# Moving GpSimd's last biases, products and sum ahead of VectorE's last split of maxima, with a new order of stores and products in the tail

## The chip, the cores and the metric

The kernel runs on one core of a Trainium2 chip. The metric is the device time of one execution in microseconds (us); a kernel is judged by the median of several executions. One further execution was taken with the hardware profiler: its span runs from its first to its last instruction, and its own time is a little longer than its span.

## The reference

A residual attention layer whose queries and keys are shifted by a projected condition; 8 batches, 512 rows, width 512, 16 heads of 32, all in float32:

```python
Q = split_heads(x @ Wq.T + bq); K = split_heads(x @ Wk.T + bk); V = split_heads(x @ Wv.T + bv)
tQ = split_heads(tokens @ Wq.T + bq); tK = split_heads(tokens @ Wk.T + bk)   # tokens = cond[:, None, :]
scores = einsum('bhqd,bhkd->bhqk', Q + tQ, K + tK) / sqrt(32)
attn = softmax(scores, axis=-1)
out = x + merge_heads(einsum('bhqk,bhkd->bhqd', attn, V))
```

## The kernel before, in words

**Steps.** The work is cut into T = 32 steps; step t is batch t // 4 and a group of four heads t % 4. A step needs, for its 128 rows of q and k (four heads of 32), the scores of 512 queries by 512 keys, their row maxima, exponentials, row sums (the denominators), and the product with V. The projections of the next batch (each product is made from seven smaller block products, as in Strassen's scheme) are spread over the steps as filler for TensorE. The main loop (L1236, function `thirds`) handles steps 1 to 28, in three thirds each. The last three steps, 29, 30 and 31, are written out by hand from L1294 to the end.

**Maxima.** The scores of step t+1 are first computed with queries on the partitions, and VectorE reduces them to negated row maxima (`nmax`, L589, L650, L1289). Before the scores of that step can be computed a second time with keys on the partitions, the maximum has to be added inside TensorE's sum. So `split_max` (L710 to L719) splits each float32 maximum into three bfloat16 pieces by four tiny dependent instructions on 128x16 elements: a cast (L716), a difference (L717), a cast (L718), a difference (L719). In the main loop GpSimd does them; for steps 30 and 31 VectorE does (L1325, L1359). Then the pieces are transposed, by a DMA (`turn_max`, L728) in the loop or by TensorE (`transpose_max`, L738, and a copy, L744) at the end, and enter the scores as a small matmul (L754, L775, L1269). Only then can step t's scores (L757, L786, L1272), the exponentials of ScalarE (L767, L796, L1287) and the products with V (L801, L817) follow.

**Kept exponentials.** For steps 1 to 29 half of the exponentials of the first computation are kept (`kept`) and turned, so that they need not be computed again: VectorE transposes 32x32 blocks (`turn_kept`, L660), and DMAs from SBUF to SBUF exchange six pairs of blocks by three moves each (`swap_kept`, L665 to L683): move 0 sets one block aside, move 1 copies its partner into its place, move 2 brings the block that was set aside into the partner's place. The n-th pair's move goes to GpSimd's own DMA queue or to SyncE's, by the condition `here`. `halves_of` (L817) multiplies the turned half with V, so it needs all moves of its step.

**The residual.** `load_residual` (L182 to L196) brings x's block for a step by four DMAs of SyncE (L191); for step 31 it only points at the transposed x that is already in SBUF. `bias_residual` (L198 to L204) adds V's bias on GpSimd. `send` (L886 to L894) transposes a step's sum on VectorE (L889), multiplies by the reciprocal of the denominator on GpSimd (L890), adds the residual on GpSimd (L891) and stores by four DMAs of SyncE (L894). `send_sums` puts VectorE's reciprocal (L1049) ahead of it.

**What sets the order.** TensorE, ScalarE, VectorE and GpSimd run the instructions in the order in which the program names them; an instruction that waits holds up all that stand behind it on its engine. SyncE's queue alone is ordered by the planner of the tile framework, from its own costs and due times, under the same dependences.

**The end by hand, before the change.** In step 29's part (L1295 to L1336): last maxima of step 30, moves 1 and 2 of the swap of step 29, the products of steps 28 and 29, VectorE's split for step 30, `send_sums(28)`, `load_residual(29)`. In step 30's part: three stretches `crossed` (L1255 to L1292), each with the maxima of step 31 for 128 queries and the scores of step 30 for 128 keys, and between them `load_residual` of 30, `bias_residual` of 31 and 29, the product and the sums of 29, GpSimd's half of the first sum of exponentials (`sum_of`, L1353, L1244), `send_sums(29)`, `bias_residual(30)`. Then comes VectorE's split for step 31 (L1359), the last one. From there on each chunk of keys is one stretch of scores, exponentials, products with V and VectorE's sums (L1244, L1246), to the denominators by `times_ones` (L827).

**The tail.** Step 30's result (`y30`) is transposed on VectorE (L1390), multiplied and added on GpSimd (L1392, L1393) and stored by four DMAs (L1398). Step 31's is kept transposed: VectorE multiplies the residual with the denominators in two halves (L1411, L1413; between them ScalarE copies the denominators, L1412), adds the product with V (L1422), TensorE transposes (L898, L1424), and VectorE divides (L1427, L1432) and two DMAs store the halves (L1438), the first on ScalarE's queue and the second on SyncE's.

Of the kernel before, what the change touches and what calls it, by code (L numbers as in the profile page):

```python
# [12 lines left out]
ALU = mybir.AluOpType  # L13
# [4 lines left out]
def kernel(  # L18
# [163 lines left out]
    def load_residual(t):  # L182

        b, g = divmod(t, G)
        if turned_by_vector(t):
            if t >= T - 3:
                xr[t] = late[0][:, (t - T + 3) * 4, :].rearrange("p (f e) -> p f e", e=BL)
            else:
                xr[t] = op.tile([P, NB, BL], F32, tag="xr", name=f"xr_{t}")
            for h in range(HG):  # L190
                nc.sync.dma_start(  # L191
                    xr[t][h * BL : (h + 1) * BL], spread(x[b], g * P + h * BL)
                )
        else:

            xr[t] = xT[b][:, g, :]  # L196
# [465 lines left out]
    APART = [(a, g) for a in range(HG) for g in range(a + 1, HG)]  # L662
    between = store[:, 16:18]

    def swap_kept(t, move, last=nc.gpsimd):  # L665

        later = 6 if t % 4 == 1 else 2

        def part(a, g):
            return kept[t][a * BL : (a + 1) * BL, g].rearrange("p c h s -> p (c h s)")  # L670

        for n, (a, g) in enumerate(APART):
            at = (n + 2) % HG * BL
            aside = (store[:, 6:8] if t == KEPT[-1] else between)[at : at + BL, n // HG]
            aside = aside.rearrange("p i s -> p (i s)")
            to, of = [(aside, part(a, g)), (part(a, g), part(g, a)), (part(g, a), aside)][move]
            if t < KEPT[-2]:
                here = move == 2 or move == 0 and n >= later
            elif t < KEPT[-1]:
                here = move == 2 and n < 3 or move == 0 and n >= later  # L680
            else:
                here = n >= 3
            (last if here else nc.sync).dma_start(to, of)  # L683

    def denominators(t, qc, w=HG, js=range(HG)):

# [36 lines left out]
    def turn_max(t):  # L723

        if t >= T:
            return
        maxT[t] = op.tile([P, S], BF16, tag="maxT", name=f"maxT_{t}")
        nc.sync.dma_start_transpose(  # L728
            maxT[t].rearrange("p (c q) -> p c q", c=NS),
            split[t % 2].rearrange("p c h e -> p (c h e)"),  # L730
        )
# [398 lines left out]
    def thirds(t, made):  # L1130

        b, r = divmod(t, G)
        of = (t - 1) // G + 1
        begin(0, HG)
        turn_more(t, 0, 0)
        row_max_aside(t + 1, 1)
        max_aside(t + 1, 1)
        row_max(t + 1, 2, False, HG)
        turn_more(t, 0, 1)
        denominators(t + 1, 1, None, (1, 2, 3, 0))  # L1140
        denominators(t + 1, 2, HG)
        weighted(t - 1, banks(0), banks(1), nothing)
        turn_more(t, 0, 2)
        load_blocks()
        one_item(of, *next(made), (2, 3), ignore, nothing)
        released(0, 1, 4, 5, 6, 7, 2, 3)
        for i in (1, 2):
            begin(HG)
            exponentials_of_rest(t, i - 1)
            turn_more(t, i, 0)  # L1150
            rows = (t + 1, 3) if i == 1 else (t + 2, 0)
            row_max(*rows, False, HG)
            turn_more(t, i, 1)
            if i == 1:
                swap_kept(t, 2)
                split_max(t + 1)
                turn_max(t + 1)
            dens = lambda js=range(HG): denominators(*rows, HG, js)
            n, u, kind = next(made)
            if kind == "first":  # L1160
                products(of, n, u, kind, False, dens, nothing, None)
                turn_more(t, i, 2)
            elif n == "v":
                small = nothing
                if t + 1 not in KEPT:
                    small = lambda: transpose_max(t + 1, banks(2), nc.scalar.copy)
                other_shared(of, n, u, dens, (0, 3), small, lambda: turn_more(t, i, 2))
                released(1, 2, 4, 5, 6, 7, 0, 3)
            else:
                products(of, n, u, kind, False, dens, nothing, False)  # L1170
                turn_more(t, i, 2)
            if i == 1:
                aparts[t] = masked(t)
            load_blocks()
            if (t + 1, i) == (KEPT[-1], 1):
                swap_kept(t + 1, 0)
            if i == 2:
                if r == 0:
                    combine_x(b + 1, 1, nc.gpsimd)
                if t + 1 < KEPT[-1]:  # L1180
                    load_residual(t + 1)
            else:
                if t > 1:
                    bias_residual(t)
                if r == 0:
                    combine_x(b + 1, 0, nc.gpsimd)
            if i == 2 and t + 1 < KEPT[-1]:
                for move in range(2):
                    swap_kept(t + 1, move)
# [35 lines left out]
    def one_item(b, n, u, product, at, dens, last):  # L1225
# [7 lines left out]
        else:  # L1233
            other_products(n, b, u, dens, nothing, at, True)

    for t in KEPT[:-1]:  # L1236
        thirds(t, iter(MADE[(t - 1) % G * 3 :]))
    places[:] = *range(8, 16), *range(4), 16, 17
# [52 lines left out]
            )  # L1291
        row_max_of(u, qc, 1, banks(HG + 2, 2))  # L1292

    late.append(store[:, 4:8].rearrange("p c i s -> p (c i) s"))  # L1294
    t = T - 3  # L1295
    begin(0, HG)
    first, second = row_of[0][:HG], row_of[0][HG:]
# [12 lines left out]
    swap_kept(t, 1)  # L1310
    apart = masked(t - 1)
    aparts[t] = masked(t)
    swap_kept(t, 2)
    halves_of(t - 1, banks(0), (1,))
    row_of[0] = [*second[:2], *first[2:], *first]
    exponentials_of_rest(t, 0)
# [14 lines left out]
    halves_of(t, banks(0), (1,), (2, 3))  # L1331
    nc.scalar.copy(whole[t][:, HS:], banks(0)[:, HS:])
    send_sums(t - 1, whole[t - 1], den)
    load_residual(t)
    at_end[:] = [*row_of[0][HG:], first[1], first[0], first[3], second[0]]
    row_of[0] = None  # L1336

# [1 line left out]
    row(0)  # L1339
    crossed(t, 0, 1)  # L1340
    apart = masked(t - 1)
    for u in (t, t + 1):
        load_residual(u)
    for u in (t + 1, t - 1):
        bias_residual(u)
    halves_of(t - 1, banks(2), (0,))
    nc.scalar.copy(whole[t - 1][:, :HS], banks(2)[:, :HS])
    spread_sums(apart, banks(1))
    den = denominators_of(t - 1, banks(1))
    row(1)  # L1350
    crossed(t, 1, 2)
    acc = room_for_sums(t)
    sum_of(t, acc, 1, nc.gpsimd, [1])  # L1353
    part_of(t, banks(2), [0])
    send_sums(t - 1, whole[t - 1], den)
    bias_residual(t)
    row(2)
    crossed(t, 2, 3)
    split_max(t + 1, nc.vector)  # L1359
# [29 lines left out]
    y30 = op.tile([P, NB, BL], F32, tag="res", name=f"res_{t - 1}")  # L1389
    nc.vector.transpose(y30.rearrange("p f e -> p (f e)"), parts[t - 1])  # L1390
    x30 = xr.pop(t - 1)
    nc.gpsimd.tensor_tensor(y30, y30, rec.broadcast_to([P, NB, BL]), ALU.mult)  # L1392
    nc.gpsimd.tensor_tensor(y30, y30, x30, ALU.add)  # L1393

    def store_30(queue, hs):
# [1 line left out]
        for h in hs:  # L1397
            queue.dma_start(spread(out[b], g * P + h * BL), y30[h * BL : (h + 1) * BL])  # L1398

    store_30(nc.sync, (0, 1, 3))  # L1400
    exponentials(t, 3, (4, 2, 0, 1))
    times_v(t, 2, pv)
    pd = bank(7)
# [6 lines left out]
    two = [slice(0, HS), slice(HS, S)]  # L1410
    nc.vector.tensor_tensor(part_x[:, two[0]], pd[:, two[0]], xr[t][:, two[0]], ALU.mult)  # L1411
    nc.scalar.copy(den, pd)  # L1412
    nc.vector.tensor_tensor(part_x[:, two[1]], pd[:, two[1]], xr[t][:, two[1]], ALU.mult)  # L1413
    store_30(nc.scalar, (2,))
    oT = late[0][:, 2, :]
    y = late[0][:, 1, :].rearrange("p (c s) -> p c s", c=NS)
    rec = op.tile([P, NS, HG, 1], F32, tag="rec", name="rec")
    pi, po = bank(6), [bank(4), bank(2)]
# [1 line left out]
    untranspose(den, pi)  # L1420
    for i in range(2):
        nc.vector.tensor_tensor(oT[:, two[i]], pv[:, two[i]], part_x[:, two[i]], ALU.add)  # L1422
        for qc in (i * 2, i * 2 + 1):
            nc.tensor.transpose(  # L1424
                po[i][:, qc * P : (qc + 1) * P], oT[:, qc * P : (qc + 1) * P], ident
            )
# [45 lines left out]
```

## Time and profile before

| | us |
|---|---|
| median of 3 runs | 659.02 (658.79 to 660.39) |
| the profiled execution's own time | 658.57 |
| its span | 656.8 |
| TensorE busy | 646.9 (98%) |
| VectorE busy | 600.8 (91%) |
| ScalarE busy | 534.6 (81%) |
| GpSimd busy | 431.1 (66%) |

In the profile PE is TensorE's matmul, PEld its weight load, DVE VectorE, ACT ScalarE, POOL GpSimd, SP SyncE; a q behind an engine's name is its sequencer, which issues DMAs. A line of the timeline has start and duration in us, engine, source line, operation, tile written and tiles read with their shapes, the count that was merged and, in brackets, the idle time before it with what ended it. The span lies 1.8 us inside the execution's own time, and the execution is 0.45 us below the median of the three runs.

### The profile page before, as it was taken

How to read it: one execution, taken by the hardware profiler on the slowest of the kernel's cores; microseconds unless marked ns; L12 is line 12 of the kernel's file. 1: busy time of each engine (PE TensorE's matmuls, PEld its weight loads, DVE VectorE, ACT ScalarE, POOL GpSimd, SP SyncE). 2: the span in 40 equal slices, each digit the busy share in tenths (PEclk: the TensorE clock that was granted, in tenths of full speed). 3: DMA queues.
4: the chain of work that ended last, by engine and by line, in shares of the span. 5: the costliest groups of instructions: out<-in, count | busy, mean ns of one | idle time of the engine just before them, and what ended most of it. 6: DMA issues, size and time to landing. Idle time of an engine off the chain costs nothing.

```text
span 656.8 us, 24923 instructions
## 1 busy us (share of the span) xinstructions
PE 646.9 (98%) x9856; PEld 349.5 (53%) x9856; DVE 600.8 (91%) x832; ACT 534.6 (81%) x1364; POOL 431.1 (66%) x680
## 2 busy tenths in 40 slices
PE   9999999999999999999999999999999999999977
PEld 7355455555555555555555555555555555555522
DVE  4799999999999999999999999999999989899897
ACT  2579888889888888988888898888898888887544
POOL 3633665796766777678757667677676776674651
PEclk9999999999999999999999999999999999999989
DMA  7633698988876787877898777787888767687521
GB/s 189 107 49 59 136 182 159 170 175 180 184 158 158 151 186 172 187 156 165 173 194 166 166 164 171 167 180 150 190 190 182 176 146 163 157 148 185 142 46 33
DMA packets 248458, 102.02 MB, mean 155 GB/s; under 512 B 229963, under 2 KB 230475, under 8 KB 248341
## 3 DMA queue, kind: packets, MB, share of 16 engines
q1 hardware_dynamic: 234724, 65.60, 52.6%
q0 software_dynamic: 12384, 33.83, 19.1%
q8 instruction: 78, 1.28, 0.9%
q10 hardware_dynamic: 1232, 0.98, 0.5%
q14 instruction: 40, 0.32, 0.2%
HBM read 19.75 MB, written 8.39 MB: 43 GB/s over the span
## 4 chain that ended last, share of the span: by engine, by line
PE 97%; DVE 1%; DMA 1%; issue 0%; ACT 0%; SPq 0%; DVEq 0%
PE psum L461 44%; PE psum L641 19%; PE psum L817 16%; PE psum L786 8%; PE psum L775 3%; PE psum L404 2%; PE psum L801 2%; PE psum L757 1%; DMA store<-in_x_dram 1%; PE psum L827 0%; PE psum L754 0%; DVE split L718 0%; PE psum L911 0%; PE psum L1272 0%; PE psum L313 0%; PE psum L852 0%
## 5 line engine op out<-in xcount | busy, mean ns | idle before, releaser
L702 ACT ACTIVATE store<-psum,nmax 128x512 f32<-128x512 f32 x204 | 140.1, 701 | 36.0 <-DVE nmax L589 26.3
L702 ACT ACTIVATE psum<-psum,nmax 128x512 f32<-128x512 f32 x248 | 164.7, 669 | 3.6 <-DVE nmax L589 3.0
L683 POOL DMA_DIRECT2D store<-store x258 | 128.7, 502 | 58.4 <-DMA store<-store 40.7
L589 DVE TENSOR_REDUCE nmax<-psum 128x1 f32<-128x512 f32 x225 | 144.4, 678 | 19.0 <-PE psum L641 16.8
L650 DVE TENSOR_REDUCE nmax<-psum 128x2 f32<-128x1024 f32 x125 | 151.4, 1211 | 0.0
L641 PE MATMUL psum<-kT,qT 32*128 32x512 f32 x1024 | 142.5, 617 | 0.0
L796 ACT ACTIVATE store<-psum 128x512 f32<-128x512 f32 x232 | 119.8, 602 | 26.7 <-PE psum L786 26.7
L660 DVE STREAM_TRANSPOSE store<-store 128x1024 f32<-128x1024 f32 x116 | 138.8, 1216 | 0.0
L817 PE MATMUL psum<-store,v 128*32 128x256 f32 x1856 | 106.8, 381 | 0.0
L817 PEld LDWEIGHTS psum<-store,v 128*32 128x32 f32 x1856 | 57.0, 110 | 57.1 <-ACT wT_q L628 21.2
L890 POOL TENSOR_TENSOR res<-res,recs 128x512 f32<-128x512 f32 x30 | 31.4, 1046 | 66.8 <-DVE res L889 66.7
L641 PEld LDWEIGHTS psum<-kT,qT 32*128 32x128 f32 x1024 | 55.7, 183 | 35.5 <-issue 20.0
L786 PE MATMUL psum<-qT,kT 32*128 32x256 f32 x928 | 59.9, 373 | 0.0
L702 ACT ACTIVATION_READ_ACCUMULATOR psum<-psum,nmax 128x1 f32 x248 | 52.7, 213 | 0.0
L461 PE MATMUL psum<-wc_v,xc 128*32 128x256 f32 x768 | 47.7, 379 | 0.0
L786 PEld LDWEIGHTS psum<-qT,kT 32*128 32x128 f32 x928 | 45.5, 184 | 3.9 <-issue 0.3
L204 POOL TENSOR_TENSOR xr<-xr,bvs 128x512 f32<-128x512 f32 x29 | 37.1, 1280 | 11.4 <-DMA x<-in_x_dram 11.4
L461 PE MATMUL psum<-xc,wc_k 128*32 128x256 f32 x720 | 44.5, 379 | 0.0
L461 PE MATMUL psum<-xc,wc_q 128*32 128x256 f32 x720 | 44.5, 379 | 0.0
L702 ACT ACTIVATION_READ_ACCUMULATOR store<-psum,nmax 128x1 f32 x204 | 43.9, 215 | 0.0
L891 POOL TENSOR_TENSOR res<-res,xr 128x512 f32<-128x512 f32 x29 | 37.1, 1278 | 2.3
L461 PE MATMUL psum<-xT,wT_k 128*32 128x256 f32 x480 | 34.5, 382 | 0.0
(196 smaller groups left out, 1001.4 us busy)
## 6 DMA issues: line engine op xcount, KB each, us to landing
store<-store SPq DMA_DIRECT2D x264, 128.0 KB, 2.6
store<-store POOLq DMA_DIRECT2D x258, 128.0 KB, 3.5
out_dram<-res SPq DMA_DIRECT2D x123, 64.0 KB, 3.6
xr<-in_x_dram SPq DMA_DIRECT2D x116, 64.0 KB, 3.0
x<-in_x_dram SPq DMA_DIRECT2D x112, 64.0 KB, 3.4
w_q<-in_L_cond_Wq_dram SPq DMA_DIRECT2D x4, 256.0 KB, 3.9
w_v<-in_L_cond_Wv_dram SPq DMA_DIRECT2D x16, 64.0 KB, 2.4
w_k<-in_L_cond_Wk_dram SPq DMA_DIRECT2D x16, 48.0 KB, 2.6
```

Source lines behind the costliest of these rows:

```text
L204: nc.gpsimd.tensor_tensor(xr[t], xr[t], bias, ALU.add)
L461: nc.tensor.matmul(pt[r], still[:, r], moving, start=(kc == kcs[0]), stop=(kc == kcs[-1]))
L589: nc.vector.tensor_reduce(nmax[t][:, qc, j : j + 1, 0], pt, AX.X, ALU.max, negate=True)
L641: nc.tensor.matmul(pt, qkT["q", t][r, qc * P : (qc + 1) * P], qkT["k", t][r, :], start=True, stop=True,)
L650: nc.vector.tensor_reduce(nmax[t][:, qc, pr * 2 : pr * 2 + 2, 0], pt, AX.X, ALU.max, negate=True)
L660: nc.vector.transpose(e, e)
L683: (last if here else nc.sync).dma_start(to, of)
L702: nc.scalar.activation(to, of, AF.Exp, bias=nmax[t][:, qc, j, :], accum_out=sums[t][:, qc, j, :],)
L786: nc.tensor.matmul(bank[j][:, i * HS : (i + 1) * HS], qkT["k", t][r, kc * P : (kc + 1) * P], qkT["q", t][r, rest], start=False, stop=(i == 1),
L796: nc.scalar.activation(e[:, i, :], bank[pr * 2 + i], AF.Exp)
L817: nc.tensor.matmul(pt[j * HD : (j + 1) * HD, half * HS : (half + 1) * HS], vs[b % 2][:, kc, (g * HG + j) * HD : (g * HG + j + 1) * HD], e, ...
L891: nc.gpsimd.tensor_tensor(y, y, xr.pop(t), ALU.add)
```

## The change

- **Residuals.** Step 29's residual gets a tile of the ordinary pool, and its load stands in the main loop's last pass; step 30's gets another place (row 2 of the late room, not row 4), and its load stands behind the swap of step 29. The output of step 31 before the transpose takes row 4 instead.
- **Biases.** `bias_residual(31)` and `bias_residual(29)` stand in step 29's part, ahead of and behind move 2 of its swap. `bias_residual(30)` stands at the end of that part, behind `send_sums(28)`.
- **Product of step 29.** `send_sums(29)` stands one `crossed` earlier, ahead of GpSimd's sum.
- **Swaps.** All six pairs' move 2 of step 28 goes to GpSimd's queue, three ahead of the split of maxima for step 29 and three behind its transpose. All six pairs' move 0 of step 29 goes to SyncE's queue.
- **Tail.** The multiplication for `y30` is VectorE's. `y30`'s stores are two on SyncE's queue and two on ScalarE's, not three and one. The product of the second half (L1413) stands behind the first half's addition (L1422).

```diff
         if turned_by_vector(t):
-            if t >= T - 3:
-                xr[t] = late[0][:, (t - T + 3) * 4, :].rearrange("p (f e) -> p f e", e=BL)
+            if t == T - 2:
+                xr[t] = late[0][:, 2, :].rearrange("p (f e) -> p f e", e=BL)
...
-    def swap_kept(t, move, last=nc.gpsimd):
+    def swap_kept(t, move, some=range(6)):
...
-        for n, (a, g) in enumerate(APART):
+        for n in some:
+            a, g = APART[n]
...
-            if t < KEPT[-2]:
+            if t < KEPT[-1]:
                 here = move == 2 or move == 0 and n >= later
-            elif t < KEPT[-1]:
-                here = move == 2 and n < 3 or move == 0 and n >= later
             else:
-                here = n >= 3
-            (last if here else nc.sync).dma_start(to, of)
+                here = move > 0 and n >= 3
+            (nc.gpsimd if here else nc.sync).dma_start(to, of)
...
             if i == 1:
-                swap_kept(t, 2)
+                first = range(6 if t + 1 < KEPT[-1] else 3)
+                swap_kept(t, 2, first)
                 split_max(t + 1)
                 turn_max(t + 1)
+                swap_kept(t, 2, range(len(first), 6))
...
-                if t + 1 < KEPT[-1]:
-                    load_residual(t + 1)
+                load_residual(t + 1)
...
     swap_kept(t, 1)
     apart = masked(t - 1)
     aparts[t] = masked(t)
+    load_residual(t + 2)
+    bias_residual(t + 2)
     swap_kept(t, 2)
+    bias_residual(t)
+    load_residual(t + 1)
     halves_of(t - 1, banks(0), (1,))
...
     send_sums(t - 1, whole[t - 1], den)
-    load_residual(t)
+    bias_residual(t + 1)
...
     apart = masked(t - 1)
-    for u in (t, t + 1):
-        load_residual(u)
-    for u in (t + 1, t - 1):
-        bias_residual(u)
     halves_of(t - 1, banks(2), (0,))
     nc.scalar.copy(whole[t - 1][:, :HS], banks(2)[:, :HS])
     spread_sums(apart, banks(1))
     den = denominators_of(t - 1, banks(1))
+    send_sums(t - 1, whole[t - 1], den)
     row(1)
     crossed(t, 1, 2)
     acc = room_for_sums(t)
     sum_of(t, acc, 1, nc.gpsimd, [1])
     part_of(t, banks(2), [0])
-    send_sums(t - 1, whole[t - 1], den)
-    bias_residual(t)
     row(2)
     crossed(t, 2, 3)
     split_max(t + 1, nc.vector)
...
-    nc.gpsimd.tensor_tensor(y30, y30, rec.broadcast_to([P, NB, BL]), ALU.mult)
+    nc.vector.tensor_tensor(y30, y30, rec.broadcast_to([P, NB, BL]), ALU.mult)
     nc.gpsimd.tensor_tensor(y30, y30, x30, ALU.add)
...
-    store_30(nc.sync, (0, 1, 3))
+    store_30(nc.sync, (0, 1))
...
     nc.scalar.copy(den, pd)
-    nc.vector.tensor_tensor(part_x[:, two[1]], pd[:, two[1]], xr[t][:, two[1]], ALU.mult)
-    store_30(nc.scalar, (2,))
-    oT = late[0][:, 2, :]
+    store_30(nc.scalar, (2, 3))
+    oT = late_part(4)
...
     for i in range(2):
         nc.vector.tensor_tensor(oT[:, two[i]], pv[:, two[i]], part_x[:, two[i]], ALU.add)
+        if i == 0:
+            nc.vector.tensor_tensor(part_x[:, two[1]], pd[:, two[1]], xr[t][:, two[1]], ALU.mult)
```

The view `late` is also made ahead of the main loop instead of behind it, which is no instruction.

More of the change, by code (lines that the diff above doesn't have):

```diff
@@ L1234, in one_item @@
             other_products(n, b, u, dens, nothing, at, True)
+    late.append(store[:, 4:8].rearrange("p c i s -> p (c i) s"))
     for t in KEPT[:-1]:
@@ L1292, in crossed @@
         row_max_of(u, qc, 1, banks(HG + 2, 2))
-    late.append(store[:, 4:8].rearrange("p c i s -> p (c i) s"))
     t = T - 3
```

## The prediction

> **What bounds the kernel now.** I read the page's chain by engine first, then the chain of waits near the end, then the timeline of that place.
>
> ```profile
> PE 97%; DVE 1%; DMA 1%; issue 0%; ACT 0%; SPq 0%; DVEq 0%
> ```
>
> TensorE sets the end of nearly everything, so work moved between the other engines counts only where TensorE waits for it. The chain of waits, in order of time (start, us, what), shows the one long stretch near the end that isn't TensorE's:
>
> ```profile
> 627.89 1.27 DVE nmax L1289 x2
> ...
> 631.73 2.30 DVE split L718
> ```
>
> From 627.89 on, until TensorE goes on at 635.10 (last row of the next fence), the end hangs on VectorE: the last maxima of step 31, then their split. Why a cast of 128x16 elements takes 2.3 us, the timeline tells:
>
> ```profile
> 617.16 0.20 DVE L716 CAST split<-nmax 128x16 bf16<-128x16 f32 x1
> ...
> 617.92 0.23 DVE L719 TENSOR_TENSOR split<-rest,split 128x16 bf16<-128x16 f32 x1
> ...
> 630.32 0.20 DVE L716 CAST split<-nmax 128x16 bf16<-128x16 f32 x1
> 630.39 1.26 POOL L204 TENSOR_TENSOR store<-store,bvs 128x512 f32<-128x512 f32 x1 [5.74 <-DMA store<-in_x_dram]
> 630.56 1.13 DVE L717 TENSOR_TENSOR rest<-nmax,split 128x16 f32<-128x16 f32 x1
> ...
> 631.62 2.34 POOL L1244 TENSOR_TENSOR acc<-store 128x1024 f32<-128x1024 f32 x1
> 631.73 2.29 DVE L718 CAST split<-rest 128x16 bf16<-128x16 f32 x1
> 633.92 1.04 POOL L890 TENSOR_TENSOR res<-res,recs 128x512 f32<-128x512 f32 x1
> 634.05 0.99 DVE L719 TENSOR_TENSOR split<-rest,split 128x16 bf16<-128x16 f32 x1
> ...
> 635.10 0.40 PE L738 MATMUL psum<-identb,split 128*128 128x128 bf16 x4 [4.00 <-DVE split L719]
> ```
>
> The split of step 30 (first two rows) runs undisturbed from 617.16 to 618.15: 0.99 us. The same four instructions for step 31 run from 630.32 to 635.04: 4.72 us. Three of them end 0.04 to 0.08 us behind a GpSimd instruction: L717 at 631.69 behind L204 (631.65), L718 at 634.02 behind L1244 (633.96), L719 at 635.04 behind L890 (634.96). So the two engines take turns by whole instructions, and GpSimd's next one gets in each time. GpSimd is busy just there because its L204 waited 5.74 us for the load of step 29's residual, with the sum, step 29's product and the bias of 30 queued behind it.
>
> The Trainium skill, page SBUF — State Buffer, section "Who interferes with whom", says that a VectorE instruction with two SBUF inputs contends with a GpSimd instruction that reads SBUF, that casts can too, and that the second one blocks until the first ends. By that rule the three waits are what must happen; the rows agree.
>
> **The change part by part.**
>
> *GpSimd's queue.* These rows price what it has to do ahead of the last split, and show where VectorE does its part of step 29's product:
>
> ```profile
> 621.25 1.04 POOL L890 TENSOR_TENSOR res<-res,recs 128x512 f32<-128x512 f32 x1 [4.22 <-DVE res L889]
> 622.37 1.29 POOL L891 TENSOR_TENSOR res<-res,xr 128x512 f32<-128x512 f32 x1
> 623.62 1.04 POOL L204 TENSOR_TENSOR xT<-xT,bvl 128x512 f32<-128x512 f32 x1
> 623.94 0.18 ACT L1044 COPY den<-psum 128x16 f32<-128x16 f32 x1
> 624.74 1.29 DVE L1289 TENSOR_REDUCE nmax<-psum 128x1 f32<-128x512 f32 x2 [1.27 <-PE psum L641]
> 627.07 0.24 DVE L1049 RECIPROCAL recs<-den 128x16 f32<-128x16 f32 x1
> 627.23 0.65 DVE L889 STREAM_TRANSPOSE res<-store 128x512 f32<-128x512 f32 x1
> ```
>
> The biases of 31 (1.04) and 29 (1.26) move into GpSimd's idle 4.22 us ahead of 621.25. If that cover failed, they would meet the split of step 30 at 617.16; that price is under the rivals. The bias of 30 (1.26) takes L204's place at 623.62 and ends at 624.9. VectorE's L1049 and L889 for step 29 move from 627.07 into its idle 1.27 us ahead of 624.74: the denominators are there at 624.12, so L889 ends at about 625.0 and L1289 starts 0.2 to 0.3 late. That costs nothing: this L1289 and the reduction behind it would end by 627.5, and the next one starts at 627.87 when TensorE's scores are done. GpSimd then multiplies (1.04) and adds (1.29) until 627.4 and sums (2.34) until 629.8, half a microsecond ahead of the split at 630.32. **The split takes 0.99 and not 4.72 us: 3.73 gained.**
>
> Not shown is the reciprocal from SBUF beside a GpSimd instruction. Its end lies between 624.4 (undisturbed) and that of the bias (624.9 and its 0.04), so up to 0.7 later with a start right behind. At that end GpSimd's sum ends at 630.5 and one instruction of the split waits some 0.3; I keep that for the range. The transpose isn't held:
>
> ```profile
> 594.46 2.32 DVE L660 STREAM_TRANSPOSE store<-store 128x1024 f32<-128x1024 f32 x2
> 594.62 1.04 POOL L890 TENSOR_TENSOR res<-res,recs 128x512 f32<-128x512 f32 x1 [2.36 <-DVE res L889]
> ```
>
> Beside GpSimd's product two transposes of twice the size took 2.32 us, no more than four of L889's 0.65. A reciprocal has one SBUF input like them, so I take its lower end too.
>
> *Behind the split.* VectorE is next: a copy, eight sums and one addition, with hardly a gap to 648.14. Two groups lose time to GpSimd's last two instructions today:
>
> ```profile
> 635.95 1.44 DVE L1244 TENSOR_TENSOR acc<-store 128x1024 f32<-128x1024 f32 x1
> ...
> 637.42 3.31 DVE L1246 TENSOR_TENSOR acc<-acc,store 128x1024 f32<-128x1024 f32 x2
> ...
> 645.80 2.34 DVE L1246 TENSOR_TENSOR acc<-acc,store 128x1024 f32<-128x1024 f32 x2
> ```
>
> Undisturbed, two sums take 2.34 and one 1.17. **So 0.27 and 0.97 go, 1.24 together.** VectorE's sums would end at 648.14 - 3.73 - 1.24 = 643.17.
>
> TensorE gains more than that behind the gap, as the window shows (the granted clock is the 0.57):
>
> ```profile
> 635.00:639.00 4.00, 3.90 (x24) 1.10 (x24) 3.40 (x4) 0.00 (x0) 3.47 (x2) 0.57 0.32 55
> ```
>
> ```profile
> 647.68 1.99 PE psum L827 x14
> ```
>
> After 4.00 us of idling it gets 0.57 of its clock; its 3.90 busy us would be 2.2 at the full one. With a gap of some 0.3 us I expect the full clock, 1.7 us for TensorE, 5.4 in all. But VectorE gains only 4.97, and the last denominators (from 647.68) already need its last sum (648.14), so VectorE's 4.97 is what counts. If the clock fell all the same, TensorE would gain the 3.73 alone and the total would be 1.2 less.
>
> The Trainium skill, page TensorE: Matmul & The Clock Gate, Part 1, says that the clock halves after an idle window of about 3.4 us and returns after a busy one. The trace agrees with its gap of 4.00; by the page a gap of 0.3 would leave the clock alone, which gives the sum as I make it.
>
> *The tail.*
>
> ```profile
> 649.77 1.05 POOL L1392 TENSOR_TENSOR res<-res,recs 128x512 f32<-128x512 f32 x1 [11.26 <-DVE res L1390]
> 650.18 0.42 DVE L1411 TENSOR_TENSOR store<-psum,xT 128x256 f32<-128x256 f32 x1 [0.49 <-PE psum L827]
> ...
> 651.25 0.42 DVE L1413 TENSOR_TENSOR store<-psum,xT 128x256 f32<-128x256 f32 x1 [0.65 <-ACT store L1412]
> ...
> 651.60 0.75 DVE L1422 TENSOR_TENSOR store<-psum,store 128x256 f32<-128x256 f32 x2
> ...
> 652.19 1.41 SPq L1398 DMA_DIRECT2D out_dram<-res  x3
> ...
> 652.61 0.75 DVE L1432 TENSOR_TENSOR store<-psum,rec 128x256 f32<-128x256 f32 x2
> 653.11 0.44 ACTq L1438 DMA_DIRECT2D out_dram<-store  x1
> 653.71 0.47 SPq L1438 DMA_DIRECT2D out_dram<-store  x1
> ```
>
> The product for `y30` on VectorE isn't shown: half of 1.17 from below, GpSimd's 1.05 from above; I take 0.6, by the same engine's row. It fills the 0.49 idle ahead of L1411 and delays it by 0.1 (0.6 at the upper end). L1413 waits 0.65 for ScalarE; L1422's first half now fills that wait, so its second half ends 0.33 sooner. The last store goes out at 653.71, 0.35 behind L1432 (653.36), because SyncE issues three stores until 653.60; ScalarE's goes out 0.08 behind its half (652.61 + 0.42). With two stores 0.27 goes. **Tail: -0.1 + 0.33 + 0.27 = 0.5 gained.**
>
> **Sum:** 3.73 + 1.24 + 0.5 = 5.5 us, so 658.57 - 5.5 = 653.1 for the profiled execution. The median of the runs shown, 659.02, lies 0.45 above that execution; between the two footings I forecast 653.3.
>
> **The rivals.** The swaps and loads add no work to TensorE, but can be late for it:
>
> ```profile
> 599.69 2.96 SPq L683 DMA_DIRECT2D store<-store  x3
> 607.46 1.52 POOL L683 DMA_DIRECT2D store<-store  x3 [6.00 <-DVE v L1206]
> 611.58 1.93 PE L817 MATMUL psum<-store,v 128*32 128x256 f32 x32
> 621.67 1.93 PE L817 MATMUL psum<-store,v 128*32 128x256 f32 x32
> 625.68 1.56 SPq L191 DMA_DIRECT2D store<-in_x_dram  x3
> ```
>
> *A transfer is late ahead of 622* (0.12). Step 28's last three moves leave SyncE (599.69) for GpSimd, behind a split; L817 at 611.58 reads them. If they go out within 3 us of where they do now, nothing waits. But GpSimd's DMA at 607.46 stood still for 6.00 us, for no reason that I find. Held likewise, the three would leave by 609.0; the loads of 625.68 to 627.24 were there at 630.39, 3.2 us behind the last issue, and with as much again for the queue TensorE would stall up to 2 us. Or the bias of 29 slips to 617 and holds the split of step 30 by its 1.26. Time: 653.3 + 1.2 to 2.0 = 654.5 to 655.3.
>
> *The change doesn't do what it says* (0.08). SyncE's order is the planner's; today it issues three loads of a residual at 625.68, and GpSimd has them at 630.39. If step 30's load goes out there, its bias, step 29's product and the sum again run from 630.39: the split's waits become 1.1, 1.0 and 1.3 and it ends 1 us sooner, L1244 gains nothing, L1246 its 0.97. With part of the tail that is hardly 2 us: 657.
>
> *Slower* (0.04). GpSimd's moves 1 of step 29 now wait for moves 0 from SyncE's queue, and its moves 2 for those; L817 at 621.67 reads them all. Today GpSimd's last leaves by 617.03 (621.25 - 4.22). The change loses from the point where this exchange ends 5.5 us behind 621.67, at 627.2. Two standstills of 6.00 us, one ahead of each move, and the 3.2 to land would bring it to 632.2, 5.0 past that point: 658.6 + 5.0 = 664. For it speaks the one standstill; against it, that GpSimd's moves from 607.46 on were all out by 617.03.
>
> **How the numbers follow.** Forecast 0.74, late transfer 0.12, no effect 0.08, slower 0.04; the remaining 0.02 lies below the forecast. The range takes in the open prices of the forecast (0.3, 0.5 and 1.2 upwards; TensorE's 0.4 beyond VectorE and as much again of the tail downwards) and the late transfer: 652.3 to 655.5. A measurement here tells about 0.3% (2 us) from no change: faster by more 0.88, within it 0.07 (mostly the second rival), slower 0.05.
>
> **What would show it.** In the profile after, L716 to L719 at the end together take 1.0 us, with no GpSimd instruction between; L738 waits under 0.5 us; the granted clock is 1.00 in the 4 us behind; L1246's pairs take 2.34; GpSimd's L1244 ends ahead of L716; the last store leaves within 0.1 us of L1432. Wrong would be: GpSimd's biases behind 627; L817 or L738 waiting for a move or a split ahead of that; VectorE's sums no longer last ahead of L827.

## The result and the profile after

| | before | after |
|---|---|---|
| median of six executions, us | 659.57 (658.79 to 662.05) | 654.86 (653.53 to 656.53) |
| ratio of the times, with its 95% interval | | 0.9919 [0.99, 0.9939] |
| the profiled execution's own time, us | 658.57 | 656.53 |
| its span, us | 656.8 | 654.7 |
| VectorE busy, us | 600.8 | 598.4 |

The kernel is 4.7 us faster by the medians. The execution that was profiled after the change is the longest of its six and gains only 2.1 us of span. Both have to be explained: the first has the direction that was forecast and falls short of its 5.5 us, the second isn't in the forecast.

Line numbers after the change differ by one in most places: the last split is L715 to L718, its transposes L737, the sums L1245 and L1247, the denominators L826. First the timeline of the changed kernel (start, duration, engine, line, what; in brackets the idle time before it) at the last split:

```profile
630.76 2.36 POOL L1245 TENSOR_TENSOR acc<-store 128x1024 f32<-128x1024 f32 x1
...
633.61 0.20 DVE L715 CAST split<-nmax 128x16 bf16<-128x16 f32 x1
633.85 0.18 DVE L716 TENSOR_TENSOR rest<-nmax,split 128x16 f32<-128x16 f32 x1
634.07 0.20 DVE L717 CAST split<-rest 128x16 bf16<-128x16 f32 x1
634.30 0.23 DVE L718 TENSOR_TENSOR split<-rest,split 128x16 bf16<-128x16 f32 x1
634.59 0.40 PE L737 MATMUL psum<-identb,split 128*128 128x128 bf16 x4 [0.20 <-DVE split L718]
635.43 1.22 DVE L1245 TENSOR_TENSOR acc<-store 128x1024 f32<-128x1024 f32 x1
636.68 2.36 DVE L1247 TENSOR_TENSOR acc<-acc,store 128x1024 f32<-128x1024 f32 x2
...
646.51 0.11 PEld L826 LDWEIGHTS psum<-acc,ones 128*32 128x32 f32 x2 [0.99 <-DVE acc L1247]
```

GpSimd's sum is over at 633.12, the split starts at 633.61, and its four instructions take 0.92 us (633.61 to 634.53) where they took 4.72. TensorE's transposes wait 0.20. The first sum and the first pair take 1.22 and 2.36, where they took 1.44 and 3.31. VectorE's last sum is still what the last denominators wait for. Next the window behind the split. A row of this view has start and end, length, then busy time and (in brackets) number of instructions of TensorE's matmuls, its weight loads, VectorE, ScalarE and GpSimd; the granted clock is the third number from the end:

```profile
635.00:639.00 4.00, 4.00 (x40) 1.05 (x40) 3.87 (x5) 3.34 (x8) 0.00 (x0) 1.00 0.01 2
```

The clock is 1.00 where it was 0.57, and TensorE gets 40 matmuls done where it did 24. Then the tail:

```profile
648.04 0.69 DVE L1391 TENSOR_TENSOR res<-res,recs 128x512 f32<-128x512 f32 x1
648.65 0.42 DVE L1410 TENSOR_TENSOR store<-psum,xT 128x256 f32<-128x256 f32 x1
...
649.33 0.42 DVE L1420 TENSOR_TENSOR store<-psum,store 128x256 f32<-128x256 f32 x1 [0.26 <-PE psum L800]
...
650.87 0.76 DVE L1432 TENSOR_TENSOR store<-psum,rec 128x256 f32<-128x256 f32 x2
...
651.69 0.41 SPq L1438 DMA_DIRECT2D out_dram<-store  x1
```

The product for `y30` takes 0.69 us on VectorE, and the last store leaves 0.06 behind L1432's end (651.63).

But the last split starts 3.29 us later than before (633.61, not 630.32). The cause lies at the split of step 30. The timeline there:

```profile
617.21 0.49 POOL L682 DMA_DIRECT2D store<-store  x1 [0.63 <-DMA store<-store]
617.38 1.68 DVE L715 CAST split<-nmax 128x16 bf16<-128x16 f32 x1
617.72 1.27 POOL L204 TENSOR_TENSOR xr<-xr,bvs 128x512 f32<-128x512 f32 x1
619.10 0.18 DVE L716 TENSOR_TENSOR rest<-nmax,split 128x16 f32<-128x16 f32 x1
...
619.91 0.49 PE L737 MATMUL psum<-identb,split 128*128 128x128 bf16 x4 [1.44 <-DVE split L718]
```

GpSimd's bias of step 29 (L204, to 618.99) runs into this split, whose cast takes 1.68 us and not 0.20. TensorE's transposes wait 1.44. The windows of one microsecond show what follows:

```profile
619.00:620.00 1.00, 0.09 (x2) 0.09 (x3) 0.83 (x5) 0.00 (x0) 0.00 (x0) 1.00 0.89 190
620.00:621.00 1.00, 1.00 (x12) 0.54 (x16) 1.00 (x3) 0.56 (x1) 0.00 (x0) 0.54 0.14 22
621.00:622.00 1.00, 1.00 (x12) 0.20 (x4) 1.00 (x2) 0.02 (x1) 0.00 (x0) 0.50 0.04 9
622.00:623.00 1.00, 1.00 (x10) 0.76 (x10) 0.87 (x3) 0.37 (x1) 0.05 (x1) 0.50 0.00 0
623.00:624.00 1.00, 1.00 (x12) 0.58 (x8) 0.02 (x1) 0.00 (x0) 0.99 (x1) 0.75 0.00 0
```

The clock falls to a half for about 3.4 us (0.46 + 0.50 + 0.50 + 0.25 lost, times two), which costs 1.7 us of TensorE's work. With the 1.44 of waiting that is 3.15. Of the 3.29, 0.23 had come ahead of all this (first column of the table below), so the two account for the other 3.06. (The cast began 0.34 ahead of the bias, while GpSimd was still issuing a DMA; which of the two held it first, the rows don't tell. It ended 0.07 behind the bias.)

To compare executions, I cut each at the same five marks, all from rows of its timeline: GpSimd's first cast of step 29's split (ahead of nearly all that is changed), the start and the end of the split for step 31, the start of VectorE's transpose of step 30's denominators (L1384, right behind its last sum) and the issue of the last store.

| profiled execution | first cast at | to the split of 31 | that split | to the transpose | to the last store | span |
|---|---|---|---|---|---|---|
| before | 600.01 | 30.31 | 4.72 | 13.03 | 5.64 | 656.8 |
| after | 600.24 | 33.37 | 0.92 | 11.84 | 5.32 | 654.7 |
| again (the same kernel) | 600.73 | 30.93 | 0.93 | 11.84 | 5.32 | 652.8 |
| `tail_only` | 600.10 | 30.30 | 5.75 | 12.96 | 5.34 | 657.5 |
| `no_tail` | 600.28 | 30.84 | 0.93 | 11.84 | 5.71 | 652.6 |
| `biases_early` | 600.93 | 30.31 | 0.93 | 11.84 | 5.32 | 652.4 |
| `early_old_swaps` | 600.81 | 31.00 | 0.92 | 11.84 | 5.31 | 653.0 |
| `gp_reads` | 600.12 | 30.30 | 5.06 | 12.79 | 5.35 | 656.7 |
| `gp_writes` | 599.97 | 30.88 | 2.29 | 11.84 | 5.31 | 653.4 |
| `old_swaps` | 600.38 | 31.63 | 0.92 | 11.84 | 5.31 | 653.1 |
| `hold_30` | 600.16 | 31.39 | 0.93 | 11.84 | 5.31 | 652.7 |
| `bias_on_act` | 600.86 | 30.31 | 0.93 | 11.84 | 5.31 | 652.3 |
| `biases_early2` | 600.26 | 30.31 | 0.92 | 11.84 | 5.31 | 651.7 |

The first column differs by 0.96 us between executions before the changed part begins; nothing can be read from a difference of that size in one span alone. Behind the last column 3.0 to 3.1 us follow in each. The changed part itself is the four columns between.

### The profile page after: what moved, and what is told of

Read it like the earlier page. It is cut to its first block, busy times and chain, and to the rows that moved or that the text cites. A ratio compares the mean times of both kernels' runs of the same rounds, so it can differ in the third digit from the quotient of the medians.

```text
span 654.7 us, 24917 instructions
## 1 busy us (share of the span) xinstructions
PE 647.7 (99%) x9856; PEld 350.3 (54%) x9856; DVE 598.4 (91%) x833; ACT 534.3 (82%) x1364; POOL 428.6 (65%) x679
## 3 DMA queue, kind: packets, MB, share of 16 engines
q8 instruction: 78, 1.28, 0.9%
## 5 line engine op out<-in xcount | busy, mean ns | idle before, releaser
L589 DVE TENSOR_REDUCE nmax<-psum 128x1 f32<-128x512 f32 x225 | 144.5, 679 | 18.9 <-PE psum L641 16.6
L204 POOL TENSOR_TENSOR xr<-xr,bvs 128x512 f32<-128x512 f32 x30 | 38.5, 1282 | 9.9 <-DMA xr<-in_x_dram 9.8
```

The source lines that it names most:

```text
L204: nc.gpsimd.tensor_tensor(xr[t], xr[t], bias, ALU.add)
L589: nc.vector.tensor_reduce(nmax[t][:, qc, j : j + 1, 0], pt, AX.X, ALU.max, negate=True)
```

## The experiments

The theory: what held the last split were GpSimd's instructions beside it, freeing it brings 3.8 us there and 1.2 in the sums, and the change loses some of this again because its bias of step 29 meets the split of step 30. The rivals: the first profile was an accident and the collision isn't the rule; the tail brings the gain; the swaps' new queues make the loss, not the bias; a wait of that length at TensorE costs little. Where nothing else is said, a diff is against the changed kernel. Where GpSimd gets extra work, it writes only where nothing is read any more.

**The same kernel again.** No edit.

> The changed kernel once more. Its first profile lost about 3 us where the bias of 29 met the split of step 30 (L715 took 1.68 us). Theory A (the bias comes late only when the exchange of blocks by DMA is late): this differs from run to run; in a run of about 654 us L715 to L718 of step 30 take 1.0 to 1.4 us together and TensorE waits under 0.5 us there. Theory B (it is the order of the queue, the same in every run): L715 again takes over 1.5 us and TensorE waits over 1 us in the profile, and the times of all runs hold that loss. Median by both: 654.0 to 655.2, ratio 0.992.

654.6 us (653.79 to 655.69, five executions), ratio to the kernel before 0.9923 [0.9909, 0.9936]. Its timeline at the split of step 30, and a window of four us behind:

```profile
617.34 1.28 POOL L204 TENSOR_TENSOR xr<-xr,bvs 128x512 f32<-128x512 f32 x1
...
617.86 0.83 DVE L715 CAST split<-nmax 128x16 bf16<-128x16 f32 x1
```

```profile
620.00:624.00 4.00, 4.00 (x56) 1.90 (x56) 4.00 (x8) 2.77 (x6) 1.34 (x2) 1.00 0.07 11
```

The collision is here too, but GpSimd's bias starts 0.52 ahead of the cast, not 0.34 behind, and so holds it by 0.6 only. The clock stays at 1.00. So neither theory holds as it stood: the collision is the rule (all four profiles with the bias at this place have it), its size and the half clock are not. The mean granted clock of each execution says the same: 0.997 in the one that was profiled first, 0.998 or more in the ten others of this kernel.

**The tail alone, and all but the tail.** `tail_only` is the kernel before with the four edits of the tail; `no_tail` is the changed kernel without them:

```diff
-    nc.vector.tensor_tensor(y30, y30, rec.broadcast_to([P, NB, BL]), ALU.mult)
+    nc.gpsimd.tensor_tensor(y30, y30, rec.broadcast_to([P, NB, BL]), ALU.mult)
...
-    store_30(nc.sync, (0, 1))
+    store_30(nc.sync, (0, 1, 3))
...
-    store_30(nc.scalar, (2, 3))
+    nc.vector.tensor_tensor(part_x[:, two[1]], pd[:, two[1]], xr[t][:, two[1]], ALU.mult)
+    store_30(nc.scalar, (2,))
...
-        if i == 0:
-            nc.vector.tensor_tensor(part_x[:, two[1]], pd[:, two[1]], xr[t][:, two[1]], ALU.mult)
```

> The kernel before with the tail's edits alone (product for y30 on VectorE, two and two stores, L1413 behind the first half's addition). Theory A (the gain is the last split): 0.3 to 0.5 us faster, ratio 0.9993, the split of step 31 still takes 4.7 us. Rival (the tail brings most of it): 3 us or more faster, ratio under 0.996.

> The changed kernel with the tail as before. Theory A: 0.3 to 0.5 us slower than the changed kernel, ratio to before 0.9925; split of step 31 in 1.0 us. Rival (the tail brings most): ratio over 0.996.

`tail_only` 659.68 us (658.56 to 661.17, twelve executions), ratio 1.0002 [0.999, 1.0013]; `no_tail` 654.47 (654.24 to 656.82, six), ratio 0.9927 [0.9913, 0.9942]. In the table the tail takes 5.31 to 5.35 us with its edits and 5.64 or 5.71 without: a gain of 0.3 to 0.4 that the medians don't show. Nearly the whole gain comes from ahead of it. `tail_only` also shows the old split once more:

```profile
630.16 1.26 POOL L204 TENSOR_TENSOR store<-store,bvs 128x512 f32<-128x512 f32 x1 [5.42 <-DMA store<-in_x_dram]
630.40 1.08 DVE L716 CAST split<-nmax 128x16 bf16<-128x16 f32 x1
...
631.52 2.25 DVE L717 TENSOR_TENSOR rest<-nmax,split 128x16 f32<-128x16 f32 x1
...
633.80 0.99 DVE L718 CAST split<-rest 128x16 bf16<-128x16 f32 x1
...
634.82 1.33 DVE L719 TENSOR_TENSOR split<-rest,split 128x16 bf16<-128x16 f32 x1
```

Here GpSimd's bias of 29 starts 0.24 ahead of the cast (before: 0.07 behind), so all four instructions are held, 5.75 us in all. The split that the change frees was itself of varying length.

**The biases ahead of move 1.** GpSimd's biases stand ahead of the moves for which it has to wait:

```diff
+    load_residual(t + 2)
+    bias_residual(t + 2)
+    bias_residual(t)
     swap_kept(t, 1)
     apart = masked(t - 1)
     aparts[t] = masked(t)
-    load_residual(t + 2)
-    bias_residual(t + 2)
     swap_kept(t, 2)
-    bias_residual(t)
```

> The changed kernel with the biases of 31 and 29 ahead of move 1 of step 29's swap, where GpSimd waited 2.43 us for a DMA. Theory A and B (the bias of 29 holds the split of step 30, and TensorE's clock falls behind it): the split of step 30 takes 1.0 us, TensorE waits under 0.3 us there, granted clock 1.00 from 620 to 624, and the median falls by 1 to 1.5 us below the changed kernel's, to 653.3 (ratio 0.990). Rival (the split of step 30 is late for the maxima or the moves, not for the bias): no change against the changed kernel.

> The kernel with early biases once more, for comparison on the same chip: by theory A 653.2 to 654.2, ratio to before 0.990 to 0.992, both splits in 1.0 us, and the product of 29 waits under 0.6 us for the exchange of blocks.

`biases_early` 653.95 us (653.24 to 654.2, four executions), ratio 0.9911 [0.9897, 0.9925]; `biases_early2`, the same kernel on another chip, 653.78 (653.5 to 653.82, four), ratio 0.9909 [0.9896, 0.9922]. The timeline of `biases_early`:

```profile
616.90 1.06 POOL L682 DMA_DIRECT2D store<-store  x2 [0.28 <-issue]
618.07 0.20 DVE L715 CAST split<-nmax 128x16 bf16<-128x16 f32 x1
...
618.84 0.23 DVE L718 TENSOR_TENSOR split<-rest,split 128x16 bf16<-128x16 f32 x1
...
628.40 2.37 POOL L1245 TENSOR_TENSOR acc<-store 128x1024 f32<-128x1024 f32 x1
631.24 0.20 DVE L715 CAST split<-nmax 128x16 bf16<-128x16 f32 x1
...
631.94 0.23 DVE L718 TENSOR_TENSOR split<-rest,split 128x16 bf16<-128x16 f32 x1
```

Both splits are free. From the first cast to the split of 31 it takes 30.31, exactly what it took before the change: the 0.6 to 3.1 us that the changed kernel loses ahead of the last split are the collision's, and this order gets them back. It has the lowest medians here. Its ratio's interval overlaps that of the changed kernel. By single executions, which come from several chips, all twelve of `biases_early`, `biases_early2` and `bias_on_act` (below) lie at 654.27 or under, and 16 of the 21 with the bias at the split of 30 (after, again, `no_tail`, `old_swaps`) above it; of `early_old_swaps` (next), whose splits are free too but where TensorE waits for a transfer, three of six lie above it.

**The swaps' queues as before,** once with the change's biases (`old_swaps`) and once with the early ones (`early_old_swaps`). Only `swap_kept` and its call in the loop are undone:

```diff
-            if t < KEPT[-1]:
+            if t < KEPT[-2]:
                 here = move == 2 or move == 0 and n >= later
+            elif t < KEPT[-1]:
+                here = move == 2 and n < 3 or move == 0 and n >= later
             else:
-                here = move > 0 and n >= 3
+                here = n >= 3
```

> The changed kernel with the moves of steps 28 and 29 on the queues of before. Theory A (the bias of 29 waits behind move 2 on GpSimd, and that is late because moves 0 come late from SyncE's queue): GpSimd's last move leaves by 617.0 as before, with two biases in front or behind, so the bias of 29 still meets the split of step 30 in part: 654 to 655.5. Rival (the new queues cause the meeting): the split of step 30 takes 1.0 us and the time is 653.5 to 654.

> The kernel with early biases (both ahead of move 1), and the moves of steps 28 and 29 on the queues of before. Theory A (only GpSimd's order ahead of the two splits counts; the new queues of the moves bring nothing): as the kernel with early biases, 653.5 to 654.5, ratio 0.990 to 0.992. Rival (the new queues are a part of the gain): 655 or more. In the profile by theory A the split of step 30 is free of GpSimd's instructions.

`old_swaps` 655.02 us (653.96 to 657.08, four executions), ratio 0.9938 [0.9917, 0.9958]; `early_old_swaps` 654.28 (653.41 to 654.85, six), ratio 0.992 [0.9904, 0.9935]. Two rows of `old_swaps`, whose line numbers are those of before:

```profile
618.28 1.55 DVE L719 TENSOR_TENSOR split<-rest,split 128x16 bf16<-128x16 f32 x1
618.46 1.27 POOL L204 TENSOR_TENSOR xr<-xr,bvs 128x512 f32<-128x512 f32 x1
```

The bias meets the split of step 30 on the old queues as well, so the rival that blames the new ones for the collision falls. But they aren't without effect. In `early_old_swaps`, where both splits are free, this stands:

```profile
619.36 0.97 POOL L683 DMA_DIRECT2D store<-store  x2 [1.68 <-DMA store<-store]
...
623.15 1.07 PE L817 MATMUL psum<-store,v 128*32 128x256 f32 x16 [0.63 <-DMA store<-store]
```

The last moves of step 29 leave GpSimd by 620.33 there, and TensorE waits 0.63 for them, most of the 0.69 by which its split of 31 comes late in the table. In `biases_early`, on the new queues, they leave by 617.96 and nothing waits. This is one profile of `early_old_swaps`; the medians of the two kernels don't separate.

**Putting the suspect back.** Three kernels add to `biases_early` instructions of GpSimd's that wait for the maxima (by a copy of four of them) and then run beside a split. `gp_reads` and `gp_writes` do it at the last split, `hold_30` at that of step 30 with one addition of 128x512:

```diff
+    scrap = [wT["k"][:, i : i + 2, :] for i in (0, 2)]
+    nc.gpsimd.tensor_copy(bvs[:, 0, :HG], nmax[t + 1][:, 3, :, 0])
+    for _ in range(2):
+        nc.gpsimd.tensor_tensor(scrap[0], scrap[0], scrap[1], ALU.add)
     split_max(t + 1, nc.vector)
```

`gp_writes` has `nc.gpsimd.memset(wT["k"][:], 0.0)` in place of the addition.

> The kernel with early biases, and on GpSimd behind its sum a copy of 4 maxima of step 31 and two additions of 128x1024 in SBUF whose result nobody uses; the copy waits for the same maxima as the split. Theory A (GpSimd's instructions that read SBUF hold the split and later VectorE's sums): the split of step 31 takes 4 to 5 us, TensorE waits 3 to 4 us ahead of the transposes of its pieces, its clock falls, and the time is 4 to 5 us longer than with early biases, about 658.5. Rival (the split was slow for its own waits on semaphores, not for GpSimd): the split takes 1.0 us and the time is that of early biases, 654.

> As the one with the additions, but GpSimd fills 128x2048 in SBUF twice, which reads nothing. Theory A with shared reading alone: the two differences take 0.2 us as ever, the casts are at most held once or twice by one fill; the whole split 1 to 3 us, time 654 to 656. Rival (any GpSimd instruction holds VectorE): three of the four are held, each to the end of a fill, and the time is that of the additions if the fills last as long.

> The kernel with early biases, and on GpSimd one copy of 4 maxima and one addition of 128x512 in SBUF that nobody uses, at the split of step 30 (the copy waits for the same maxima). Theory A (the bias of 29 cost the changed kernel its time by holding this split for the rest of one such instruction): the split takes about 2.2 us, TensorE waits 1.2 to 1.5 us ahead of the transposes of its pieces, the time is 1.2 us longer than with early biases, and some 2.7 us longer in executions in which TensorE's clock also falls behind the wait (mean granted clock under 0.998). Rival (there is slack behind the split of step 30): under 0.5 us longer.

`gp_reads` 659.62 us (658.33 to 660.31, ten executions), ratio 0.9999 [0.9988, 1.001]: the whole gain is gone. Its timeline:

```profile
630.42 0.20 DVE L715 CAST split<-nmax 128x16 bf16<-128x16 f32 x1
...
630.61 4.78 POOL L1361 TENSOR_TENSOR wT_k<-wT_k 128x1024 f32<-128x1024 f32 x2
630.66 2.32 DVE L716 TENSOR_TENSOR rest<-nmax,split 128x16 f32<-128x16 f32 x1
633.02 0.20 DVE L717 CAST split<-rest 128x16 bf16<-128x16 f32 x1
633.26 2.22 DVE L718 TENSOR_TENSOR split<-rest,split 128x16 bf16<-128x16 f32 x1
...
635.54 0.40 PE L737 MATMUL psum<-identb,split 128*128 128x128 bf16 x4 [4.34 <-DVE split L718]
...
640.86 0.69 DVE L1375 TENSOR_TENSOR parts<-psum,parts 128x512 f32<-128x512 f32 x1 [0.87 <-PE psum L800]
```

Each difference ends with one of GpSimd's two additions (they are merged in one row, 2.39 each). Nothing of the program waits for these additions; they cost by being there. Behind the wait of 4.34 the clock is at 0.50 from 635.90 to 639.31, and VectorE, whose sums nothing holds here (1.22 for one and 2.36 for the first pair), waits 0.87 for a product of TensorE's (last row). `gp_writes`, 654.93 us (654.62 to 657.6, four executions), ratio 0.9941 [0.992, 0.9963], is another picture:

```profile
631.02 3.66 POOL L1361 MEMSET wT_k<- 128x2048 f32 x2
631.09 0.19 DVE L716 TENSOR_TENSOR rest<-nmax,split 128x16 f32<-128x16 f32 x1
631.31 1.56 DVE L717 CAST split<-rest 128x16 bf16<-128x16 f32 x1
632.91 0.23 DVE L718 TENSOR_TENSOR split<-rest,split 128x16 bf16<-128x16 f32 x1
```

Beside a fill, which reads nothing, the differences take 0.19 and 0.23; the cast between them is held to the end of the first fill (631.02 + 1.83 = 632.85). `hold_30` 654.84 us (654.23 to 656.02, six executions), ratio 0.9929 [0.9916, 0.9942], against 653.78 for `biases_early2`, measured together with it on the same chip: one GpSimd addition of 1.26 us at the split of step 30 costs 1.06 us of the median, a little under the 1.2 expected, which is the price of a hold of that length by itself:

```profile
617.51 1.26 POOL L1330 TENSOR_TENSOR wT_k<-wT_k 128x512 f32<-128x512 f32 x1
617.54 1.27 DVE L716 TENSOR_TENSOR rest<-nmax,split 128x16 f32<-128x16 f32 x1
...
619.44 0.40 PE L737 MATMUL psum<-identb,split 128*128 128x128 bf16 x4 [1.04 <-DVE split L718]
```

**A bias less on GpSimd.** In `biases_early`, ScalarE adds the bias of step 31, behind a copy of its own:

```diff
-    bias_residual(t + 2)
...
+    nc.scalar.activation(xr[t + 2], xr[t + 2], AF.Identity, bias=bvl)
```

> The kernel with early biases, the bias of 31 not on GpSimd but on ScalarE, in its idle time behind the copy of step 28's product. Theory A with the exchange close to its due time: moves 1 and 2 of step 29 leave GpSimd up to 1.0 us sooner, no stall ahead of the last product of 29, 0 to 0.5 us shorter than early biases. Rival (SyncE's moves 0 bind the exchange): no difference; ScalarE's exponentials may come 0.1 later.

654.06 us (653.2 to 654.27, four executions), ratio 0.9912 [0.9898, 0.9925]; `biases_early2`, measured together with it, has 653.78. GpSimd's last move leaves 16.6 us behind the first cast, between the 17.0 of `biases_early` and the 16.3 of `biases_early2`, so no sooner than it does anyway, and nothing was waiting for it. No gain.

## Why the prediction came out as it did, point by point

- **The split** (3.73 gained, 0.99 left). 3.80 gained; 0.92 or 0.93 left in every profiled execution without GpSimd beside it. Shown both ways: freed by the change, and held again in `gp_reads`.
- **The sums** (1.24). From the split's end to the transpose 13.03 became 11.84, 1.19. The size is right, but the runs show that it isn't due to freed sums alone. In `gp_reads` the sums are free and the clock is at a half, and the stretch takes 12.79; so sums that are freed while the clock still falls bring some 0.2, and the rest needs the full clock. The prediction had this as its case of a fallen clock, 1.2 less in total.
- **The clock** (no half clock behind a gap of 0.3, and TensorE's gain not counted, as VectorE's sums end last). The gap is 0.20, the clock 1.00, and the last denominators still wait 0.99 for a sum. Right.
- **The reciprocal beside GpSimd** (0 to 0.7, taken as 0). In the changed kernel GpSimd was idle at that place. In `biases_early2` it ran beside a bias of 1.28 us that started at 623.86, and took its usual time:

```profile
624.40 0.25 DVE L1048 RECIPROCAL recs<-den 128x16 f32<-128x16 f32 x1 [0.68 <-ACT den L1043]
```

- **The tail** (0.5). 0.32 (5.64 to 5.32). The store's part was right (0.06 behind L1432); the product for `y30` takes 0.69, not 0.6, and the first addition (L1420) now waits 0.26 for a product of TensorE's. The term of the tail was sized 0.2 too high.
- **GpSimd's queue: the step that failed.** The prediction said that the biases of 31 and 29 "move into GpSimd's idle 4.22 us ahead of 621.25" and costed that at nothing. The bias of 31 ran earlier, at 614.31 between two of the moves, and met no split. The bias of 29 stands behind move 2, whose last DMA leaves at 617.03 by the prediction's own figure, and the split of step 30 begins at 617.16. The idle stretch was the stretch of that split. So the collision needed no slip at all; it was the normal case. I gave it as part of a rival with a chance of 0.12 and a time of 654.5 to 655.3, and that is where the medians came out (654.86 and 654.6), not at 653.3. That they lie so near the forecast is partly luck: the collision costs little beside the 5.5 us, but the order of events that the sum assumes didn't occur in this kernel. The forecast's order of events is that of `biases_early`, and there the sum holds: 658.57 less 653.5 for `biases_early2` is 5.07, and its later start (0.25) makes 5.32, against 5.5.
- **The price of the collision.** The 1.26 that the prediction gave for it left out the clock. It was 0.62 in one profiled execution (30.93 less 30.31), 3.06 in the other, of which the half clock is 1.7.
- **The late transfer.** Step 28's moves on GpSimd's queue were no trouble: TensorE is busy for 12.00 of the 12 us from 604 to 616. Step 29's exchange has little to spare: its last move leaves 16.3 to 17.0 us behind the first cast where both splits are free and nothing waits, and where it left 19.5 behind it, TensorE waited 0.63. In the changed kernel the wait at the split and the half clock already make up the delay, so the rival that ends slower came nowhere near. (`gp_writes`, whose last move left 17.7 behind its first cast, has 0.57 in the table that I can't place: TensorE waits 0.51 ahead of the product of step 29's turned half, and the trace names ScalarE as the releaser.)
- **No effect** fell: the load of step 30's residual is out in time (SyncE issues its last three parts at 616.08), and GpSimd's bias of 30 starts at 625.31, not 630.39.
- **The footing.** Six executions of the kernel before give 659.57, and three later measurements 659.83, 658.94 and 659.92, not 659.02. Without the collision the new kernel lies at 653.78 and 653.95, half a microsecond over the forecast. The tail is 0.2 of that; that the rest is the start of the part, which came 0.25 and 0.92 later in these two than in the profile I worked from, is argued. The collision adds 0.65 where both were measured together (654.6 over 653.95). That the old split's varying length (4.72 and 5.75 in two profiles) and the clock behind it lift the old kernel's median over its profiled execution fits the clocks on record, but isn't shown: of the 45 executions in the three later measurements, the ten with a mean granted clock of 0.994 or less take 659.49 to 661.25, and the 18 with 0.996 or 0.997 have a median of 658.84, with some up to 660.19. Single executions of `no_tail`, `old_swaps` and `gp_writes` took 656.82, 657.08 and 657.6 at clocks of 0.999 or more; no trace shows why.

## What to carry to other kernels

Before an operation is put into an engine's idle stretch, lay the other engines' rows of that same stretch beside it: the idle time that looked free here was just the time of the next short critical chain on the engine that shares with it. Where a queue waits for DMAs, put work that needs none of them ahead of the wait, not behind it; then its time doesn't depend on theirs. And when one profiled execution is far from its median, cut several executions at the same marks before anything is explained by their spans.

## What the runs showed of the hardware that was not expected

- **Which short VectorE instruction is held depends on what GpSimd does.** Differences with two SBUF inputs: 2.32 and 2.22 us beside GpSimd's additions, 0.19 and 0.23 beside its fills. A cast: 1.56 beside a fill. A reciprocal: 0.25 beside a bias, not held. The Trainium skill, page SBUF — State Buffer, section "Who interferes with whom", says that two SBUF inputs contend with a GpSimd instruction that reads but not with one that only writes, and that casts can contend; these rows agree with it.
- **The half clock behind a short idle time, and how long it lasts.** A wait of 1.44 us at 618.5 to 619.9 was followed by a clock of 0.50 from 620.08 to 623.50. Waits of 1.28 and 1.04 us at the same place (`old_swaps`, `hold_30`), and of 1.56 at the last split (`gp_writes`), left it at 1.00. So the length alone doesn't decide, within these lengths. The half clock lasted 3.42 us here, 3.42 in the kernel before (635.38 to 638.80), 3.41 in `gp_reads` and 6.83, twice as much, in `tail_only`. There it began at 633.26, in the middle of TensorE's wait (631.2 to 636.2), so it starts with neither end of an idle stretch. The Trainium skill, page TensorE: Matmul & The Clock Gate, Part 1, has the clock fall after an idle window of about 3.4 us that runs freely. The steps of 3.4 us agree with such a window, but it need not be idle throughout: in the 3.42 us ahead of 620.08 TensorE was busy for 1.98. How busy is busy enough, no run here shows; that waits of 1.28 and 1.56 were split between two windows is an obvious reading, not a shown one.
- **A standing GpSimd queue.** In the kernel before, its DMA at 607.46 stood for 6.00 us, for which the prediction found no reason. The trace names VectorE's L1206 as the releaser; it ends at 607.40, 0.06 ahead of the DMA. The same stands in `early_old_swaps` (6.00, DMA at 608.25, 0.07 behind the same sum), and on the new queues, where other moves come first, the first DMA stands 3.15 (at 604.62). Why a DMA that copies kept exponentials waits for a sum of v stays open.
- **Executions differ by up to 0.96 us** at a mark which the changes hardly touch (599.97 to 600.93), and by 0.67 between two of the same kernel (`biases_early` and `biases_early2`). What makes it wasn't looked into.
